# A second norm's statistics as sums, one product for delta*u, and a projection in two column tiles

## The chip, the cores and the metric

The kernel runs on one core of a Trainium2 chip. The metric is the device time of one execution in microseconds (us), median of several runs. A core has five engines, each with its own queue of instructions that it works off in order: TensorE (PE in the profile, with PEld for its weight loads), VectorE (DVE), ScalarE (ACT), GpSimd (POOL) and SyncE (SP), which here only issues DMAs. Engines wait for one another by semaphores. All data is float32.

## The reference, cut to what matters

Two layers follow one another. The first is a Mamba block over a picture of 128 x 128 pixels read as a sequence of 16384 steps, for 4 pictures (the batch), followed by a group norm, a SiLU and a residual. The second norms its input again, and uses that only to get four mixing weights for a filter in the frequency domain.

```python
# layer 0
u = silu(conv(x_in) + conv_b)                       # 256 channels
x_dbl = u @ x_proj_w.T                              # 8 + 16 + 16 = 40 columns
dt, Bm, Cm = split(x_dbl, [8, 24])
delta = softplus(dt @ dt_proj_w.T + dt_proj_b)
h = h * exp(delta * A) + delta * B * u              # scan over 16384 steps, 256 x 16 states
y = einsum('bds,bs->bd', h, C)
...
x = silu(group_norm(out, 4 groups)) + x             # first norm
# layer 1
a = group_norm(concat([x, x]), 32 groups)           # second norm: mean and variance of the line above
weights = softmax(mean(relu(a @ agg_w + agg_b)) @ wg_w.T + wg_b)
out = irfft2(sum_f weights_f * rfft2(x) * rfft2(filtered_f(x))) + 0.5 * x
```

What the change touches is the projection of `u` to 40 columns, the product `delta * u`, and the mean and variance of the second norm. The result of the computation stays the same but for rounding.

## The kernel before

**Tiling.** `block0` cuts each picture into 32 chunks of 512 steps, so 128 chunks `k` in all (`NCH` = 32 for a picture). Per chunk there are 256 channels x 16 states = 4096 state rows, laid out as 32 tiles of 128 partitions x 512 steps. The tiles are called by `(j, r, p)`: `j` is the half of the channels (2), `r` the rotation (4), `p` the group of states (4). Two tiles make a pair, and there are `NP` = 16 pairs per chunk, one for each step of the schedule. So step `n` of the whole program is pair `n % 16` of chunk `n // 16`.

**What one tile costs.** ACT makes `da = exp(delta * A)` (L393). The input `delta*u*B` of the scan is made on POOL for `p` = 1, 2, 3 (`dbu`, L363) and by PE and ACT for `p` = 0 (`bt_act` L304, `dbu_turn` L383). DVE runs the scan over the 512 steps (L412). Then `h` is multiplied by `C`: on DVE (L414) where `by_vector(k, j, r, p)` says so, on POOL (L419) otherwise. ACT copies the last column for the next chunk (`st`, L415 and L420). PE adds the products up to `y` (`sums`, L433), DVE multiplies `y` by the gate (L443).

**The share of h*C.** As `by_vector` stands, DVE multiplies the tiles with `p` = 2 and 3, 16 of 32. In odd chunks it takes one more, (1, 2, 1). In chunks in which the norm of the previous picture runs (`norming(k)`, L338: `k >= 32` and `k % 32` from 2 to 17, so 16 chunks for each of three pictures, 48 in all) DVE takes one less, without (1, 2, 2), which is pair 13.

**Order.** The order is written out by hand. `pre(k)` and `post(k)` list triples of step, phase and function. Step 0 of `pre` is the first pair of the chunk before (`pre` runs one chunk ahead). In each step the phases come in the order of L552: turn, sums, pe, exps, late, act, pool, dbu, early, gate, scans, dve, end. Every engine gets its instructions in that order. What the change touches runs thus, with steps counted within a chunk:

- step 2: `silu_act` (u), and in norming chunks two `norm_act` (L633: SiLU of the first norm, written to PSUM)
- step 3: `xd_mm` (L247: u times the 40 columns), and at the end of the step two `norm_dve` (L637: plus the residual, then the store) each followed by `norm_stats` (L641: `bn_stats`)
- step 4: `xd_act` (L253: the copy of the 40 x 512 result, and the store of B and C to DRAM)
- step 5: `dt_mm` (L267), `xd_turn` (L282: four transposes of 40 x 128), the loads of B and C, and `o_act` (L456, L457) of an earlier chunk
- step 6: `dt_act` (L275: softplus[...]); step 7: `xd_turn_act` (L286), `du_pool` twice on POOL (L312, with a store each); step 8: `du_turn` (L293); step 9 and 16: `rep_load` (the loads of delta and delta*u, each repeated four times over the partitions)

The exponentials for the pairs are spread over this: `exps(n)` puts the first tile of an even pair three steps early, and everything else in the step before its scan.

**The norms.** `finish` runs both norms of one picture beside the chunks of the next picture. `group_norm` is used for the first one (`which` = 0, sums and sums of squares from ACT, L456 and L457) and for the second (`which` = 1, `bn_stats` and `bn_aggr`). The last picture has no chunks left to hide behind. Its `finish` runs in `block1`, the frequency part, where DVE, ACT and POOL have other work.

Of the kernel before, what the change touches and what calls it, by code (L numbers as in the profile page):

```python
# [26 lines left out]
F32 = mybir.dt.float32  # L27
AF = mybir.ActivationFunctionType
ALU = mybir.AluOpType
AX = mybir.AxisListType  # L30
# [3 lines left out]
P = 128  # L34
# [12 lines left out]
def kernel(ctx: ExitStack, tc: tile.TileContext, a: dict, out: bass.AP):  # L47
# [32 lines left out]
    def first_constants(s):  # L80

        s.b1 = col("mlp_b1")
        s.w2 = const("w2", [P, NH, C], a["mlp_w2T"].rearrange("(j p) c -> p j c", p=P))
        s.b2 = col("mlp_b2")
        win = s.win = const("win", [P, 2 * DI], a["in_wT"])
        wck = s.wck = const("wck", [P, KC, DI], a["conv_wT"].partition_broadcast(P))
        s.cb = col("conv_b")
        s.wx = const("wx", [P, NH, NX], a["x_wT"].rearrange("(j p) r -> p j r", p=P))
        s.wdt = const("wdt", [R, DI], a["dt_wT"])
        s.bdt = col("dt_b")  # L90
        s.ident = const("ident", [P, P], a["c_ident"])
# [63 lines left out]
def block0(tc, s):  # L155
    nc, B, NCH, NH, NS, NG, ND, R, NX, KC, HALO, C, L, NF, DI = (
        s.nc, s.B, s.NCH, s.NH, s.NS, s.NG, s.ND, s.R, s.NX, s.KC, s.HALO, s.C, s.L, s.NF, s.DI,
    )
    NT = T // P
    with ExitStack() as ctx:  # L160
        def pool(name, bufs, **kw):
            return ctx.enter_context(tc.tile_pool(name=name, bufs=bufs, **kw))
# [3 lines left out]
        hpool = pool("hb", 4)  # L166
        tiny = pool("tiny", 2)
        dbc = pool("dbc", 2, space=DRAM)
        s.spare = p2
# [14 lines left out]
        def pre(k):  # L184
# [59 lines left out]
            def xd_mm():  # L244
                ps["xd"] = turn_bank(f"xd_{k}")
                for j in range(NH):
                    nc.tensor.matmul(  # L247
                        ps["xd"][0:NX, :], s.wx[:, j, :], d["u"][:, j, :], start=j == 0, stop=j == NH - 1
                    )

            def xd_act():
                xd = d["xd"] = p1.tile([NX, T], F32, tag="xd", name=f"xd_{k}")
                nc.scalar.copy(xd, ps["xd"][0:NX, :])  # L253
                bc = d["bc"] = dbc.tile([2, NS, T], F32, tag="bc", name=f"bc_{k}")
                nc.sync.dma_start(out=bc.rearrange("q s t -> (q s) t"), in_=xd[R:NX, :])

            def bc_load():
                for q, tag in enumerate("BC"):
# [19 lines left out]

            def xd_turn():
                ps["xt"] = turned(f"xdt_{k}")  # L280
                for t in range(NT):
                    nc.tensor.transpose(ps["xt"][:, t, 0:NX], d["xd"][:, t * P : (t + 1) * P], s.ident[0:NX, 0:NX])  # L282

            def xd_turn_act():
                d["xdt"] = p1.tile([P, NT, NX], F32, tag="xdt", name=f"xdt_{k}")
                nc.scalar.copy(d["xdt"], ps["xt"][:, :, 0:NX])  # L286

            def du_turn(h):
                ps["dut"] = turned(f"dut_{k}_{h}")
# [15 lines left out]
                        d["bt"][:, 2 * h + t, :, q, :], src, AF.Copy, scale=d["xdt"][:, 2 * h + t, R + q : R + q + 1]  # L305
                    )

            def du_pool(j):
                if j == 0:
                    d["du"] = p1.tile([P, NH, T], F32, tag="du", name=f"du_{k}")  # L310
                du = d["du"][:, j, :]
                nc.gpsimd.tensor_tensor(du, d["delta"][:, j, :], d["u"][:, j, :], ALU.mult)  # L312
                nc.sync.dma_start(out=d["dd"][1, j * P : (j + 1) * P, :], in_=du)

            def rep_load(j):
                for q, tag in enumerate(("delta", "du")):
# [9 lines left out]
                (5 if k else 7, "act", bc_load), (6, "act", dt_act), (7, "act", xd_turn_act), (7, "pool", partial(du_pool, 0)),  # L326
                (7, "pool", partial(du_pool, 1)), (8, "pe", partial(du_turn, 0)), (9, "act", partial(rep_load, 0)),
# [19 lines left out]
        def by_vector(k, j, r, p):  # L347

            if norming(k):
                return p > 1 and (j, r, p) != (1, 2, 2)  # L350
            return p > 1 or (k % 2 == 1 and (j, r, p) == (1, 2, 1))

        def dbu(u):
# [200 lines left out]
                        f()  # L554


def group_norm(s, io, b, mat, which, stat, at, then):


    nc = s.nc  # L560
    g = {}

    def small(n, m=1):
        g[n] = io.small.tile([P, m], F32, tag=n, name=f"{n}_{which}_{b}")
        return g[n]

    def aggregate():
        mv = small("mv", 2)
        if which:
            nc.vector.bn_aggr(mv, stat().rearrange("p n q -> p (n q)"))  # L570
        else:
            nc.vector.reduce_sum(mv, stat(), axis=AX.X)

    def mean_mm():
        if which == 0:
            mv, q = g["mv"], small("q")
            nc.scalar.activation(q, mv[:, 0:1], AF.Square, scale=1.0 / s.L)
            nc.scalar.mul(q, q, -1.0)
            nc.scalar.mul(mv[:, 0:1], mv[:, 0:1], 1.0 / s.L)
            nc.scalar.activation(mv[:, 1:2], mv[:, 1:2], AF.Identity, scale=1.0 / s.L, bias=q)  # L580
        ps = g["ps"] = io.psum(f"gm_{which}_{b}")
        nc.tensor.matmul(ps[:, 0:1], getattr(s, mat), g["mv"][:, 0:1], start=True, stop=True)

    def spread_act():
        mv = g["mv"]
        nc.scalar.copy(small("mean"), g["ps"][:, 0:1])
        q = small("q")
        nc.scalar.activation(q, mv[:, 0:1], AF.Square, scale=-1.0, bias=g["mean"])
        nc.scalar.activation(q, q, AF.Identity, bias=mv[:, 1:2])

    def var_mm():
        ps = g["ps"] = io.psum(f"gv_{which}_{b}")
        nc.tensor.matmul(ps[:, 0:1], getattr(s, mat), g["q"], start=True, stop=True)

    def root_act():
        nc.scalar.activation(small("rstd"), g["ps"][:, 0:1], AF.Sqrt, bias=s.eps)

    def invert():
        nc.vector.reciprocal(g["rstd"], g["rstd"])
# [8 lines left out]
def finish(s, io, b, first, norm, agg, add="dve"):  # L608

# [6 lines left out]
    def start(mean, rstd):  # L616
        for n in ("scale", "bias"):
            g[n] = io.small.tile([P, 1], F32, tag=n, name=f"{n}_{b}")
        nc.scalar.activation(g["scale"], s.gnw, AF.Identity, scale=rstd)
        nc.scalar.activation(g["bias"], mean, AF.Identity, scale=g["scale"])  # L620
        nc.scalar.activation(g["bias"], g["bias"], AF.Identity, scale=-1.0, bias=s.gnb)
        g["stat"] = io.small.tile([P, NCH, 6], F32, tag="stats1", name=f"stats1_{b}")

    def norm_load(i):
        xr = g["x", i] = io.big.tile([P, T], F32, tag="xr", name=f"xr_{b}_{i}")
# [7 lines left out]
        nc.scalar.activation(g["n", i], g["o", i], AF.Silu, bias=g["bias"], scale=g["scale"])  # L633

    def norm_dve(i):
        o = g["o", i]
        nc.vector.tensor_add(o, g.pop(("n", i)), g.pop(("x", i)))  # L637
        nc.sync.dma_start(out=s.x1flat[b][:, i * T : (i + 1) * T], in_=o)

    def norm_stats(i):  # L640
        nc.vector.bn_stats(g["stat"][:, i, :], g.pop(("o", i)))  # L641

    def middle(mean, rstd):
        g["mean"] = mean
# [51 lines left out]
    def weights_act():  # L696
        nc.scalar.activation(s.wts[b], g["lg"], AF.Identity, scale=g["total"])

    todo = group_norm(s, io, b, "g0", 0, lambda: stats[b], first, start)
# [7 lines left out]
    todo += group_norm(s, io, b, "g1", 1, lambda: g["stat"], c, middle)  # L707
    todo += [(c + 7, "pe", bias_mm), (c + 8, "act", bias_act)]
    for i in range(NCH):
        at = agg(i)  # L710
# [11 lines left out]
def block1(tc, s):  # L722
# [10 lines left out]
    with ExitStack() as ctx:  # L733
# [32 lines left out]

        t1 = norm(NCH - 1)[2] + 14
        todo = defaultdict(list)
        steps = finish(s, io, B - 1, 0, norm, lambda i: (t1 + i - 3, t1 + i, t1 + i, None), "add")
# [289 lines left out]
```

## Time and profile before

| | |
|---|---|
| median of 3 runs | 7132.03 us (7131.95 to 7132.24) |
| the profiled execution | 7134.96 us, of which the span is 7133.1 us |
| DVE busy | 6888.6 us |
| POOL busy | 6892.0 us |
| ACT busy | 6140.8 us |
| PE busy | 5887.2 us |

The span goes from the first to the last instruction of the profiled execution. The remaining 1.9 us lie around it. The chunks of `block0` take the first 6420 us or so, and the frequency part takes the rest. A group of instructions in the profile carries its line in the kernel, the engine, the output and inputs, the shape, the count, and then the busy time and the mean duration of one. On DVE, ACT and POOL a duration reaches over the start of the next instruction, so the distance from start to start is shorter than the duration. Where instructions follow one another without idle time, the distance is the price.

### The profile page before, as it was taken

What the parts mean: (1) busy time and instruction counts of PE and PEld (TensorE: products, weight loads), DVE (VectorE), ACT (ScalarE), POOL (GpSimd) and SP (SyncE); (2) the same over time, 40 slices, a digit from 0 to 9 for tenths busy, and PEclk for the clock granted to TensorE, in tenths of its full rate; (3) what the DMA queues carried; (4) which work ended last, traced back from release to release, by engine and by line L of the source; (5) the groups of instructions that cost most, each with busy time, mean ns of one, the idle gap of its engine ahead of it and who ended that gap; (6) DMA issues with size and microseconds to landing.
All of it is one profiled execution on the core that took longest, in us unless ns stands there. A gap on an engine that the chain in (4) does not pass through costs nothing.

```text
span 7133.1 us, 91388 instructions
## 1 busy us (share of the span) xinstructions
PE 5887.2 (83%) x26708; PEld 2606.0 (37%) x26708; DVE 6888.6 (97%) x7966; ACT 6140.8 (86%) x13658; POOL 6892.0 (97%) x3188
## 2 busy tenths in 40 slices
PE   6888888888887788888888888888888888877899
PEld 2333333323222233333333333333333333326789
DVE  6999999999999999999999999999999999997888
ACT  6888888888888888898888888898888888877887
POOL 6999999999999999999999999999999999997898
PEclk8888888888888889998898899998889899989999
DMA  6666666667777776777777777677777767759977
GB/s 140 159 154 162 159 151 164 160 151 176 180 188 182 182 172 170 180 180 172 195 186 196 188 175 178 168 187 173 197 189 195 190 167 177 172 140 271 274 213 209
DMA packets 909640, 1288.33 MB, mean 181 GB/s; under 512 B 81736, under 2 KB 360912, under 8 KB 909136
## 3 DMA queue, kind: packets, MB, share of 16 engines
q1 hardware_dynamic: 908992, 1282.22, 72.4%
q8 instruction: 210, 3.44, 0.2%
q14 instruction: 294, 2.41, 0.1%
q10 hardware_dynamic: 144, 0.26, 0.0%
HBM read 1025.58 MB, written 256.58 MB: 180 GB/s over the span
## 4 chain that ended last, share of the span: by engine, by line
DVE 44%; ACT 30%; issue 11%; PE 6%; DMA 4%; POOL 3%; SPq 1%; DVEq 0%; ACTq 0%; POOLq 0%
DVE da L412 20%; DVE h L412 12%; ACT da L393 12%; DVE hb L414 5%; ACT L393 3%; DMA rdelta<-dd 2%; ACT L275 2%; ACT delta L275 2%; ACT bt L304 2%; PE y L433 1%; DVE zs L443 1%; POOL hb L363 1%; ACT L242 1%; DVE pr L894 1%; POOL hb L419 1%
## 5 line engine op out<-in xcount | busy, mean ns | idle before, releaser
L363 POOL TENSOR_TENSOR hb<-rdu,rB 128x1536 f32<-128x1536 f32 (+2 forms) x1536 | 3604.8, 2363 | 22.4 <-DMA rdelta<-dd 21.3
L393 ACT ACTIVATE da<-rdelta,amat 128x512 f32<-128x512 f32 x4096 | 2794.1, 700 | 138.3 <-DVE h L412 133.9
L419 POOL TENSOR_TENSOR hb<-h,rC 128x1024 f32<-128x1024 f32 (+1 forms) x1072 | 2434.0, 2273 | 89.1 <-DVE h L412 73.8
L412 DVE TENSOR_TENSOR_SCAN da<-da,st,hb 128x512 f32<-128x512 f32 x1976 | 2419.9, 1267 | 21.4 <-ACT da L393 14.3
L433 PE MATMUL y<-hb,sel 128*32 128x512 f32 x8192 | 1314.2, 717 | 2.9 <-POOL hb L419 2.7
L414 DVE TENSOR_TENSOR hb<-da,rC 128x512 f32<-128x512 f32 x2040 | 1296.3, 674 | 3.0
L412 DVE TENSOR_TENSOR_SCAN h<-da,st,b 128x512 f32<-128x512 f32 x992 | 1258.4, 1269 | 1.8 <-PE b L383 1.6
L412 DVE TENSOR_TENSOR_SCAN h<-da,st,hb 128x512 f32<-128x512 f32 x1000 | 1251.8, 1256 | 1.8 <-ACT da L393 1.8
L383 PE MATMUL b<-ident,bt 128*128 128x128 f32 x4096 | 747.3, 305 | 517.1 <-DVE h L412 391.7
L234 PE MATMUL pp_cv<-xm,wck 128*128 128x512 f32 x2048 | 1013.5, 640 | 1.6 <-ACT xm L217 0.8
L304 ACT ACTIVATE bt<-pt_dut,xdt 128x256 f32<-128x256 f32 x2048 | 839.4, 474 | 184.5 <-PE pt_dut L293 184.3
L383 PEld LDWEIGHTS b<-ident,bt 128*128 128x128 f32 x4096 | 530.8, 154 | 1017.6 <-DVE h L412 691.6
L415 ACT COPY st<-da 128x1 f32<-128x1 f32 x2040 | 273.2, 160 | 474.5 <-DVE hb L414 471.4
L234 PEld LDWEIGHTS pp_cv<-xm,wck 128*128 128x128 f32 x2048 | 395.5, 203 | 651.9 <-issue 422.5
L830 POOL TENSOR_TENSOR wb<-wb,term 128x1040 f32<-128x1040 f32 x192 | 461.3, 2403 | 39.0 <-ACT term L824 29.6
L293 PE MATMUL pt_dut<-ident,du 128*128 128x128 f32 x1024 | 232.1, 337 | 287.7 <-ACT xdt L286 176.3
L429 PE MATMUL y<-u,diag 128*128 128x512 f32 x512 | 303.0, 675 | 187.6 <-DVE zs L443 186.1
L293 PEld LDWEIGHTS pt_dut<-ident,du 128*128 128x128 f32 x1024 | 131.9, 162 | 606.9 <-POOL du L312 478.4
L393 ACT ACT_TABLE_LOAD x262 | 336.1, 1283 | 12.0 <-DMA rdelta<-dd 7.4
L312 POOL TENSOR_TENSOR du<-delta,u 128x512 f32<-128x512 f32 x256 | 318.7, 1266 | 28.1 <-ACT delta L275 28.1
L223 PE MATMUL pp_z<-xm,win 128*128 128x512 f32 x512 | 274.5, 634 | 51.8 <-ACT fq L497 46.2
L267 PE MATMUL pp_dt<-xd,wdt 8*128 8x512 f32 x512 | 284.9, 641 | 33.2 <-ACT pp_o L457 23.5
(160 smaller groups left out, 8095.7 us busy)
## 6 DMA issues: line engine op xcount, KB each, us to landing
rdelta<-dd SPq DMA_DIRECT2D x1024, 256.0 KB, 4.6
rdu<-dd SPq DMA_DIRECT2D x1024, 256.0 KB, 7.4
rC<-bc SPq DMA_DIRECT2D x512, 256.0 KB, 7.4
rB<-bc SPq DMA_DIRECT2D x512, 192.0 KB, 4.7
dd<-delta SPq DMA_DIRECT2D x256, 256.0 KB, 7.2
dd<-du SPq DMA_DIRECT2D x256, 256.0 KB, 5.7
ft<-in_filt_w SPq DMA_DIRECT2D x108, 520.0 KB, 7.2
ob<-o SPq DMA_DIRECT2D x128, 256.0 KB, 2.1
```

Of the source, the lines that this page charges most:

```text
L234: nc.tensor.matmul(ps["cv", j], w, d["xm"][:, t : t + T], start=t == 0, stop=t == KC - 1)
L293: nc.tensor.transpose(ps["dut"][:, 2 * t + j, :], d["du"][:, j, at : at + P], s.ident)
L304: nc.scalar.activation(d["bt"][:, 2 * h + t, :, q, :], src, AF.Copy, scale=d["xdt"][:, 2 * h + t, R + q : R + q + 1])
L312: nc.gpsimd.tensor_tensor(du, d["delta"][:, j, :], d["u"][:, j, :], ALU.mult)
L363: nc.gpsimd.tensor_tensor(hb[:, p : p + n, :], d["du", j][:, m : m + n, :], d["B"][:, p - 1 : p - 1 + n, :], ALU.mult)
L383: nc.tensor.transpose(b[:, t * P : (t + 1) * P], src, s.ident)
L393: nc.scalar.activation(da, d["delta", j][:, m, :], AF.Exp, scale=s.amat[:, c : c + 1])
L412: nc.vector.tensor_tensor_scan(o, das[q], b, init, ALU.mult, ALU.add)
L414: nc.vector.tensor_tensor(hb[:, p + q, :], das[q], d["C"][:, p + q, :], ALU.mult)
L419: nc.gpsimd.tensor_tensor(hb[:, ps, :], h[:, q, :], d["C"][:, ps, :], ALU.mult)
L433: nc.tensor.matmul(y[m * DG : (m + 1) * DG, :], s.sel, d["hb", j, r][:, p, :], start=False, stop=r == NG - 1)
L830: nc.gpsimd.tensor_tensor(wb, wb, u[n].terms[f], ALU.add)
```

## The change

Three things are changed, and one share is moved to go with the first.

- **Second norm.** For the first three pictures, `norm_dve` becomes one `tensor_tensor_reduce`, which adds the residual and also sums up the result over the 512 steps. `bn_stats` is gone. ACT squares the result with a sum (`norm_stats`), one step later, in the act phase of step 4. It writes the squares over the tile of x, which nothing reads any more. `bn_aggr` becomes a `reduce_sum`, and `mean_mm` divides by the length in four small ACT instructions as it does for the first norm. The picture in `block1` keeps `bn_stats` (`sums=False`).
- **Share of h*C.** In odd norming chunks DVE takes tile (1, 2, 2) back from POOL. In the order of instructions that is 24 products of 128x512 that leave POOL and 24 that DVE gets.
- **delta*u.** One POOL product of 128x1024 and one store of 512 KB in place of two of each.
- **Projection.** `wx` is padded with zeros from 40 to 64 columns. The 512 steps are cut in two halves, whose results land on partitions 0 to 63 and 64 to 127 of PSUM, 256 columns each. So the copy to SBUF is 128x256, not 40x512, the store of B and C is two DMAs, `dt_mm` reads all 128 partitions with weights that are zero but for the rows of one half, and `xd_turn` needs two transposes, not four.

```diff
-        s.wx = const("wx", [P, NH, NX], a["x_wT"].rearrange("(j p) r -> p j r", p=P))
-        s.wdt = const("wdt", [R, DI], a["dt_wT"])
+        s.wx = s.own.tile([P, NH, P // 2], F32, tag="wx", name="wx")
+        nc.vector.memset(s.wx, 0.0)
+        nc.sync.dma_start(out=s.wx[:, :, 0:NX], in_=a["x_wT"].rearrange("(j p) r -> p j r", p=P))
+        s.wdt = s.own.tile([P, 2, DI], F32, tag="wdt", name="wdt")
+        nc.vector.memset(s.wdt, 0.0)
+        for h in range(2):
+            nc.sync.dma_start(out=s.wdt[h * P // 2 : h * P // 2 + R, h], in_=a["dt_wT"])
...
                 for j in range(NH):
-                    nc.tensor.matmul(
-                        ps["xd"][0:NX, :], s.wx[:, j, :], d["u"][:, j, :], start=j == 0, stop=j == NH - 1
-                    )
+                    for h in range(2):
+                        o = ps["xd"][h * HP : (h + 1) * HP, 0:TH]
+                        u = d["u"][:, j, h * TH : (h + 1) * TH]
+                        nc.tensor.matmul(o, s.wx[:, j, :], u, start=j == 0, stop=j == NH - 1)
...
-                xd = d["xd"] = p1.tile([NX, T], F32, tag="xd", name=f"xd_{k}")
-                nc.scalar.copy(xd, ps["xd"][0:NX, :])
+                xd = d["xd"] = p1.tile([P, TH], F32, tag="xd", name=f"xd_{k}")
+                nc.scalar.copy(xd, ps["xd"][:, 0:TH])
...
-                    nc.tensor.matmul(
-                        ps["dt", j], s.wdt[:, j * P : (j + 1) * P], d["xd"][0:R, :], start=True, stop=True
-                    )
+                    for h in range(2):
+                        o = ps["dt", j][:, h * TH : (h + 1) * TH]
+                        nc.tensor.matmul(o, s.wdt[:, h, j * P : (j + 1) * P], d["xd"], start=True, stop=True)
...
-                for t in range(NT):
-                    nc.tensor.transpose(ps["xt"][:, t, 0:NX], d["xd"][:, t * P : (t + 1) * P], s.ident[0:NX, 0:NX])
+                for t in range(2):
+                    nc.tensor.transpose(ps["xt"][:, t, :], d["xd"][:, t * P : (t + 1) * P], s.ident)
...
-            def du_pool(j):
-                if j == 0:
-                    d["du"] = p1.tile([P, NH, T], F32, tag="du", name=f"du_{k}")
-                du = d["du"][:, j, :]
-                nc.gpsimd.tensor_tensor(du, d["delta"][:, j, :], d["u"][:, j, :], ALU.mult)
-                nc.sync.dma_start(out=d["dd"][1, j * P : (j + 1) * P, :], in_=du)
+            def du_pool():
+                du = d["du"] = p1.tile([P, NH, T], F32, tag="du", name=f"du_{k}")
+                nc.gpsimd.tensor_tensor(du, d["delta"], d["u"], ALU.mult)
+                nc.sync.dma_start(out=d["dd"][1].rearrange("(j p) t -> p j t", p=P), in_=du)
...
             if norming(k):
-                return p > 1 and (j, r, p) != (1, 2, 2)
+                return p > 1 and (k % 2 == 1 or (j, r, p) != (1, 2, 2))
...
     def aggregate():
         mv = small("mv", 2)
-        if which:
+        if sums:
+            nc.vector.reduce_sum(mv, stat(), axis=AX.X)
+        else:
             nc.vector.bn_aggr(mv, stat().rearrange("p n q -> p (n q)"))
-        else:
-            nc.vector.reduce_sum(mv, stat(), axis=AX.X)
...
     def norm_dve(i):
-        o = g["o", i]
-        nc.vector.tensor_add(o, g.pop(("n", i)), g.pop(("x", i)))
+        o, n = g["o", i], g.pop(("n", i))
+        if sums:
+            total = g["stat"][:, 0, i : i + 1]
+            nc.vector.tensor_tensor_reduce(o, n, g["x", i], 1.0, 0.0, ALU.add, ALU.add, total)
+        else:
+            nc.vector.tensor_add(o, n, g.pop(("x", i)))
         nc.sync.dma_start(out=s.x1flat[b][:, i * T : (i + 1) * T], in_=o)
 
     def norm_stats(i):
-        nc.vector.bn_stats(g["stat"][:, i, :], g.pop(("o", i)))
+        o = g.pop(("o", i))
+        if sums:
+            nc.scalar.activation(g.pop(("x", i)), o, AF.Square, accum_out=g["stat"][:, 1, i : i + 1])
+        else:
+            nc.vector.bn_stats(g["stat"][:, i, :], o)
...
-            (at[2], add, partial(norm_dve, i)), (at[2], "end", partial(norm_stats, i)),
+            (at[2], add, partial(norm_dve, i)), (at[2] + sums, "act" if sums else "end", partial(norm_stats, i)),
```

More of the change, by code (lines that the diff above doesn't have):

```diff
@@ L158, in block0 @@
     )
-    NT = T // P
+    NT, TH, HP = T // P, T // 2, P // 2
     with ExitStack() as ctx:
@@ L168, in block0 @@
         dbc = pool("dbc", 2, space=DRAM)
-        s.spare = p2
+        s.own, s.spare = p1, p2
         psp = pool("psp", 2, space=PSUM)
@@ L246, in xd_mm @@
                 for j in range(NH):
-                    nc.tensor.matmul(
-                        ps["xd"][0:NX, :], s.wx[:, j, :], d["u"][:, j, :], start=j == 0, stop=j == NH - 1
-                    )
+                    for h in range(2):
+                        o = ps["xd"][h * HP : (h + 1) * HP, 0:TH]
+                        u = d["u"][:, j, h * TH : (h + 1) * TH]
+                        nc.tensor.matmul(o, s.wx[:, j, :], u, start=j == 0, stop=j == NH - 1)
             def xd_act():
-                xd = d["xd"] = p1.tile([NX, T], F32, tag="xd", name=f"xd_{k}")
-                nc.scalar.copy(xd, ps["xd"][0:NX, :])
+                xd = d["xd"] = p1.tile([P, TH], F32, tag="xd", name=f"xd_{k}")
+                nc.scalar.copy(xd, ps["xd"][:, 0:TH])
                 bc = d["bc"] = dbc.tile([2, NS, T], F32, tag="bc", name=f"bc_{k}")
-                nc.sync.dma_start(out=bc.rearrange("q s t -> (q s) t"), in_=xd[R:NX, :])
+                rows = bc.rearrange("q s t -> (q s) t")
+                for h in range(2):
+                    nc.sync.dma_start(out=rows[:, h * TH : (h + 1) * TH], in_=xd[h * HP + R : h * HP + NX])
             def bc_load():
@@ L266, in dt_mm @@
                     ps["dt", j] = psum(f"dt_{k}_{j}")
-                    nc.tensor.matmul(
-                        ps["dt", j], s.wdt[:, j * P : (j + 1) * P], d["xd"][0:R, :], start=True, stop=True
-                    )
+                    for h in range(2):
+                        o = ps["dt", j][:, h * TH : (h + 1) * TH]
+                        nc.tensor.matmul(o, s.wdt[:, h, j * P : (j + 1) * P], d["xd"], start=True, stop=True)
             def dt_act():
@@ L280, in xd_turn @@
                 ps["xt"] = turned(f"xdt_{k}")
-                for t in range(NT):
-                    nc.tensor.transpose(ps["xt"][:, t, 0:NX], d["xd"][:, t * P : (t + 1) * P], s.ident[0:NX, 0:NX])
+                for t in range(2):
+                    nc.tensor.transpose(ps["xt"][:, t, :], d["xd"][:, t * P : (t + 1) * P], s.ident)
             def xd_turn_act():
                 d["xdt"] = p1.tile([P, NT, NX], F32, tag="xdt", name=f"xdt_{k}")
-                nc.scalar.copy(d["xdt"], ps["xt"][:, :, 0:NX])
+                src = ps["xt"][:, 0:2, :].rearrange("p t (h r) -> p h t r", h=2)
+                nc.scalar.copy(d["xdt"].rearrange("p (h t) r -> p h t r", h=2), src[:, :, :, 0:NX])
             def du_turn(h):
@@ L325, in pre @@
                 (NP - 2, "pe", z_mm), (NP - 1, "act", z_act), (NP + 2, "act", z_silu), (3, "pe", xd_mm), (4, "act", xd_act), (5, "pe", dt_mm), (5, "pe", xd_turn),
-                (5 if k else 7, "act", bc_load), (6, "act", dt_act), (7, "act", xd_turn_act), (7, "pool", partial(du_pool, 0)),
-                (7, "pool", partial(du_pool, 1)), (8, "pe", partial(du_turn, 0)), (9, "act", partial(rep_load, 0)),
+                (5 if k else 7, "act", bc_load), (6, "act", dt_act), (7, "act", xd_turn_act), (7, "pool", du_pool),
+                (8, "pe", partial(du_turn, 0)), (9, "act", partial(rep_load, 0)),
                 (8, "pool", partial(bt_act, 0, 0, 1)), (9, "act", partial(bt_act, 0, 1, 5)),
@@ L554, in block0, with group_norm @@
                         f()
-def group_norm(s, io, b, mat, which, stat, at, then):
+def group_norm(s, io, b, mat, which, stat, at, then, sums):
     nc = s.nc
@@ L568, in aggregate @@
         mv = small("mv", 2)
-        if which:
+        if sums:
+            nc.vector.reduce_sum(mv, stat(), axis=AX.X)
+        else:
             nc.vector.bn_aggr(mv, stat().rearrange("p n q -> p (n q)"))
-        else:
-            nc.vector.reduce_sum(mv, stat(), axis=AX.X)
     def mean_mm():
-        if which == 0:
+        if sums:
             mv, q = g["mv"], small("q")
@@ L605, in group_norm, with finish @@
     ]
-def finish(s, io, b, first, norm, agg, add="dve"):
+def finish(s, io, b, first, norm, agg, add="dve", sums=True):
     nc, NCH, C, L, NF = s.nc, s.NCH, s.C, s.L, s.NF
@@ L621, in start @@
         nc.scalar.activation(g["bias"], g["bias"], AF.Identity, scale=-1.0, bias=s.gnb)
-        g["stat"] = io.small.tile([P, NCH, 6], F32, tag="stats1", name=f"stats1_{b}")
+        shape = [P, 2, NCH] if sums else [P, NCH, 6]
+        g["stat"] = io.small.tile(shape, F32, tag="stats1", name=f"stats1_{b}")
     def norm_load(i):
@@ L635, in norm_dve @@
     def norm_dve(i):
-        o = g["o", i]
-        nc.vector.tensor_add(o, g.pop(("n", i)), g.pop(("x", i)))
+        o, n = g["o", i], g.pop(("n", i))
[4 more added lines that the diff above has]
+            nc.vector.tensor_add(o, n, g.pop(("x", i)))
         nc.sync.dma_start(out=s.x1flat[b][:, i * T : (i + 1) * T], in_=o)
     def norm_stats(i):
-        nc.vector.bn_stats(g["stat"][:, i, :], g.pop(("o", i)))
+        o = g.pop(("o", i))
+        if sums:
+            nc.scalar.activation(g.pop(("x", i)), o, AF.Square, accum_out=g["stat"][:, 1, i : i + 1])
+        else:
+            nc.vector.bn_stats(g["stat"][:, i, :], o)
     def middle(mean, rstd):
@@ L697, in weights_act @@
         nc.scalar.activation(s.wts[b], g["lg"], AF.Identity, scale=g["total"])
-    todo = group_norm(s, io, b, "g0", 0, lambda: stats[b], first, start)
+    todo = group_norm(s, io, b, "g0", 0, lambda: stats[b], first, start, True)
     for i in range(NCH):
@@ L703, in finish @@
             (at[0], "pe", partial(norm_load, i)), (at[1], "act", partial(norm_act, i)),
-            (at[2], add, partial(norm_dve, i)), (at[2], "end", partial(norm_stats, i)),
+            (at[2], add, partial(norm_dve, i)), (at[2] + sums, "act" if sums else "end", partial(norm_stats, i)),
         ]
     c = at[2] + 5
-    todo += group_norm(s, io, b, "g1", 1, lambda: g["stat"], c, middle)
+    todo += group_norm(s, io, b, "g1", 1, lambda: g["stat"], c, middle, sums)
     todo += [(c + 7, "pe", bias_mm), (c + 8, "act", bias_act)]
@@ L768, in block1 @@
         todo = defaultdict(list)
-        steps = finish(s, io, B - 1, 0, norm, lambda i: (t1 + i - 3, t1 + i, t1 + i, None), "add")
+        steps = finish(s, io, B - 1, 0, norm, lambda i: (t1 + i - 3, t1 + i, t1 + i, None), "add", False)
         for at, phase, f in steps:
```

## The prediction

> **What bounds the kernel now.** I read the busy row of the page first, then the stretches of single chunks, then the groups of DVE, and last the order in time of ACT within one chunk.
>
> ```profile
> span 7133.1 us, 91388 instructions
> PE 5887.2 (83%) x26708; PEld 2606.0 (37%) x26708; DVE 6888.6 (97%) x7966; ACT 6140.8 (86%) x13658; POOL 6892.0 (97%) x3188
> ...
> core 0: us, PE busy (x) PEld busy (x) DVE busy (x) ACT busy (x) POOL busy (x), PEclk, DMA share, GB/s
> 632.00:680.80 48.80, 41.03 (x152) 15.52 (x152) 48.77 (x51) 41.70 (x94) 47.93 (x23) 0.84 0.65 155
> 680.80:729.50 48.70, 38.82 (x152) 14.20 (x152) 48.70 (x52) 42.03 (x96) 48.70 (x23) 0.89 0.69 161
> 2031.10:2081.40 50.30, 38.88 (x150) 13.85 (x149) 50.27 (x54) 43.25 (x95) 50.05 (x24) 0.86 0.73 184
> 2081.40:2131.70 50.30, 42.58 (x153) 15.67 (x152) 50.27 (x54) 43.25 (x95) 50.06 (x24) 0.81 0.75 185
> ```
>
> Two engines at 97% leave open which one bounds. The stretches answer it. The first two are chunk-long stretches without a norm, the last two are norming chunks (40 and 41). In all four DVE is idle for at most 0.03 us. POOL has 0.8 us in every second plain stretch and 0.25 us in a norming chunk, and ACT has 7 us. So a chunk lasts as long as DVE's work, 48.75 us plain and 50.30 us norming, and POOL stands 0.5% behind it. What is taken from POOL alone is worth nothing; what is taken from DVE is worth its price until POOL or a late ACT takes over.
>
> ```profile
> L412 DVE TENSOR_TENSOR_SCAN da<-da,st,hb 128x512 f32<-128x512 f32 x1976 | 2419.9, 1267 | 21.4 <-ACT da L393 14.3 <-POOL hb L363 4.1 <-issue 2.9
> L414 DVE TENSOR_TENSOR hb<-da,rC 128x512 f32<-128x512 f32 x2040 | 1296.3, 674 | 3.0
> ...
> 2043.52 1.28 DVE L637 TENSOR_TENSOR of<-pp_n,xr 128x512 f32<-128x512 f32 x2
> 2044.71 1.27 DVE L641 BATCH_NORM_STATS2 stats<-of 128x6 f32<-128x512 f32 x2
> 2045.90 1.26 DVE L412 TENSOR_TENSOR_SCAN h<-da,st,b 128x512 f32<-128x512 f32 x1
> ```
>
> The groups give durations (674 ns for a product), the times from start to start give prices: two additions 1.19 us, two statistics 1.19 us, so 0.595 us each. The same reading gives 0.59 for a product on DVE, 1.18 for a scan. On POOL it gives 2.31 for 128x1024 and 2.44 for the two du products.
>
> The third reading is ACT in the steps behind the norm (chunk 40), against the scan that waits for it:
>
> ```profile
> 2047.46 0.57 ACT L253 COPY xd<-pt_xd 40x512 f32<-40x512 f32 x1
> 2048.38 0.69 ACT L393 ACTIVATE da<-rdelta,amat 128x512 f32<-128x512 f32 x1 [0.34 <-DVE h L412]
> ...
> 2051.32 0.16 ACT L415 COPY st<-da 128x1 f32<-128x1 f32 x1 [0.34 <-DVE hb L414]
> 2051.91 0.16 ACT L415 COPY st<-da 128x1 f32<-128x1 f32 x1 [0.43 <-DVE hb L414]
> 2051.97 1.31 ACT L393 ACTIVATE da<-rdelta,amat 128x512 f32<-128x512 f32 x2
> ...
> 2058.86 1.30 ACT L393 ACTIVATE da<-rdelta,amat 128x512 f32<-128x512 f32 x2
> ...
> 2060.06 2.44 DVE L412 TENSOR_TENSOR_SCAN da<-da,st,hb 128x512 f32<-128x512 f32 x2
> ```
>
> ACT waits for DVE three times, 0.34 + 0.34 + 0.43 us, the last time at the copies of pair 5. From there it works without a wait through softplus and two table loads to the exponentials of pair 9 (2058.86). The first of those ends at 2058.86 + 0.69 = 2059.55, and DVE wants it at 2060.06. So ACT is only 0.51 us ahead there. The rule: if DVE gets more than that ahead of ACT, it waits at pair 9.
>
> [...] here L457, a square between exponentials, has no table load.
>
> **The change part by part.** There are 48 norming chunks with two norm pieces each.
>
> *Statistics, DVE.* Gone: two `bn_stats`, 1.19 us. Added: what the addition with a sum costs above the plain one, and two reads of the accumulator. The trace shows neither. The first is bounded by 0 (it reads the same two streams) and by 0.585 (the rate of the scan); I take 0[...]. [...]
>
> *Share of h*C.* In 24 odd chunks DVE gets a product, 0.59 us, at pair 13, behind the place in question. Mean 0.30 us per norming chunk. POOL loses 1.22 us in these.
>
> *Squares, ACT.* Two of 128x512 with their reads. L457 does the same at 0.515 us from start to start, its read at 0.09, so 2 x 0.61 = 1.21 us. They stand in step 4 behind `xd_act`, and wait for an addition that ended 3 us before, so for nothing. Behind them on ACT are one exponential, `o_act`, an early exponential, the copies of pair 5, then the softplus stretch. The xd copy shrinks by 256 columns: copies of 512 (L228) and 160 (L286) take 0.477 and 0.183 from start to start, so 0.84 ns per column and 0.21 us.
>
> *The sum at pair 9.* Before, ACT reaches the exponential of 2048.38 at 2048.04. Now it gets there at 2048.04 + 1.21 - 0.21 = 2049.04 and need not wait. Then 2.60 us of work lead to the first copy of pair 5 (2051.64), two copies take 0.16, and the exponentials of pair 7 begin at 2051.80, 0.17 earlier than before. DVE would be 1.04 earlier. The difference of 0.87 goes against the 0.51 us of lead, so DVE waits about 0.36 us at pair 9, and 0.68 of the 1.04 us remain. The other places have more lead: 1.68 us at pair 4, 1.35 at pair 5 (both in front of the squares), 1.5 at pair 7, 1.0 at pair 8. As ACT limits, a dearer addition costs nothing up to 0.18 us each.
>
> A norming chunk then takes 50.30 - 0.68 + 0.30 = 49.92 us on average, and 48 x 0.38 = 18 us are gained.
>
> *POOL.* delta*u as one product saves 2.44 - 2.31 = 0.13 us in every chunk. POOL's work in a norming chunk becomes 49.92 in even and 48.70 in odd ones, 49.3 on average, below DVE's 49.9. The even chunks lie above DVE's share by about 0.3 us; the scans stand at least 1.4 us behind the POOL products they read in chunks 36 to 47, which carries it to the next chunk. Without the moved share POOL would be the bound at 49.92 throughout. In plain chunks POOL's saving is hidden by DVE: nothing. Only late in the run does DVE wait for POOL (4.1 us in all at L363): about 1 us.
>
> *delta*u, the stores.* SP issues both halves one behind the other before the loads of delta anyway, and the loaded delta*u lies there 4 us before its use, so the merged store costs nothing. If that cover went, it would be one store of 256 KB later, a few us per chunk.
>
> *Projection.* PE is 83% busy and behind nobody here: `dt_mm` ends at 2051.5 and softplus starts at 2054.6. Whether the two column tiles run together is not seen in this trace, and is worth 0 to 1 us of 1.9 us on PE per chunk that nobody waits for (DVE's waits for PE are 43 us at the start and little else). The second store of B and C, 64 KB in all, is issued with 2 us to spare. The two memsets at the start hold up SP's loads of constants by up to 1 us, once.
>
> *End of the second norm.* `bn_aggr` (0.92 us) becomes a sum (0.13), and four ACT instructions of 0.1 to 0.2 us come in step 8, behind the exponentials of pair 9. Three times: 1 to 2 us gained.
>
> Sum: 18 + 1 + 1.5 - 0.5 = 20 us, 0.28% of the profiled 7134.96, and of the median of 7132.03, which lies 2.9 us below that one execution. Forecast 7111 us.
>
> **The rivals.**
>
> *ACT keeps up.* If the squares are cheaper or hide in waits, DVE keeps the whole 1.04 us: 48 x (1.04 - 0.30) = 36, with the rest 38 us, 7094 us. For it: ACT has 7 us idle per chunk. Against it: that idle time lies in other steps.
>
> *ACT costs more.* The squares read SBUF; the SiLU of the norm, which also does, takes 0.75 us from start to start (with two operands per partition that the square lacks). At 0.75 the squares cost 0.47 more, DVE keeps 0.21 of the 1.04 us, the moved share takes 0.30, and nothing is left: 7118 to 7134 us, no difference to be told.
>
> *The addition with a sum runs at the scan's rate.* Slower: each costs 0.585 more, so DVE's chunk is 50.30 - 1.04 + 1.17 + 0.30 = 50.73, and 48 x 0.43 = 20 us are lost, 7150 us with the 2 us of the rest. The place is step 3 of the norming chunks; with the moved share in it, loss begins at 0.37 us more per addition. For it: one known operation of this engine runs so, and this one is not in the trace. [...]
>
> **How the numbers follow.** Forecast 0.50 (7104 to 7118), ACT keeps up 0.22 (7092 to 7103), ACT costs more 0.16, slow addition 0.12. Predicted is 7111. The range leaves out the slow addition and little else: 7093 to 7132. A measurement can tell 0.2%, 14 us, from no change: faster is below 7117.8, slower above 7146.3. Faster is the forecast but for its upper end and the second case, 0.69; same 0.19; slower 0.12.
>
> **What would show it.** DVE's rows should have 96 additions of about 680 ns and 96 reads below 0.1 us, and 24 more products. Norming chunks should last 49.6 to 49.7 us even and about 50.2 odd, with idle time of 0.3 to 0.4 us before the scan of pair 9, ended by ACT's L393; plain chunks should stay at 48.7 to 48.8. The forecast is wrong if that idle time is missing (then the chunk is shorter), if additions take over a microsecond, or if POOL has no idle time left in the norming chunks.

## The result

| | before | changed |
|---|---|---|
| median of 7 runs | 7131.95 us | 7107.63 us |
| lowest and highest | 7130.78 and 7133.24 | 7105.26 and 7110.93 |
| profiled execution | 7134.96 us | 7106.15 us |
| its span | 7133.1 us | 7104.4 us |

The ratio is 0.9966, with a 95% interval of 0.9957 to 0.9976. The change is 24 us faster, or 0.34%. The two profiled executions lie 29 us apart. That is more than the medians show, because the one of before was 3.0 us above its median and the other 1.5 us below.

The page of the changed kernel, busy row first, and then the stretches of chunks 40 (even) and 41 (odd), in which the norm runs:

```profile
span 7104.4 us, 93142 instructions
PE 5622.1 (79%) x27476; PEld 2693.8 (38%) x27476; DVE 6847.9 (96%) x7992; ACT 6168.4 (87%) x13862; POOL 6845.8 (96%) x3036
...
2026.81:2076.31 49.50, 36.54 (x155) 14.60 (x155) 49.20 (x54) 43.97 (x99) 49.30 (x23) 0.89 0.74 188
2076.31:2126.26 49.95, 40.05 (x160) 16.72 (x159) 49.69 (x55) 44.03 (x99) 49.95 (x22) 0.88 0.76 186
```

The columns of the stretches are the length, then busy time of PE, PEld, DVE, ACT and POOL. Both chunks lasted 50.30 us before. DVE now has 0.3 us of idle time in each, where it had 0.03. So something else than DVE's own work sets part of the chunk. The timelines of DVE and ACT in chunk 40 say what it is:

```profile
2039.81 0.68 DVE L647 CUSTOM_DVE_ANT_0 of<-pp_n,xr 128x512 f32<-128x512 f32 x1
2040.42 0.08 DVE L647 DVE_READ_ACCUMULATOR2_ANT stats<- 128x1 f32 x1
2040.42 1.27 DVE L419 TENSOR_TENSOR_SCAN h<-da,st,b 128x512 f32<-128x512 f32 x1
...
2053.40 1.25 DVE L419 TENSOR_TENSOR_SCAN h<-da,st,hb 128x512 f32<-128x512 f32 x1
2054.92 2.47 DVE L419 TENSOR_TENSOR_SCAN da<-da,st,hb 128x512 f32<-128x512 f32 x2 [0.26 <-ACT da L400]
```

```profile
2043.14 0.36 ACT L259 COPY xd<-pt_xd 128x256 f32<-128x256 f32 x1
2043.41 0.62 ACT L655 ACTIVATE xr<-of 128x512 f32<-128x512 f32 x1
2043.93 0.19 ACT L655 ACTIVATION_READ_ACCUMULATOR xr<-of 128x1 f32 x1
2044.03 0.62 ACT L655 ACTIVATE xr<-of 128x512 f32<-128x512 f32 x1
2044.55 0.19 ACT L655 ACTIVATION_READ_ACCUMULATOR xr<-of 128x1 f32 x1
2044.64 0.68 ACT L400 ACTIVATE da<-rdelta,amat 128x512 f32<-128x512 f32 x1
...
2047.13 0.20 ACT L422 COPY st<-da 128x1 f32<-128x1 f32 x2
2047.31 1.30 ACT L400 ACTIVATE da<-rdelta,amat 128x512 f32<-128x512 f32 x2
...
2054.20 1.30 ACT L400 ACTIVATE da<-rdelta,amat 128x512 f32<-128x512 f32 x2
```

Three things are to be seen. The addition with a sum takes 0.61 us from start to start, and its accumulator read takes nothing: the scan starts at the same 2040.42 as the read, and so does the next instruction behind all 96 reads of the trace. ACT no longer waits at the copies of pair 5 (2047.13), where it waited 0.34 and 0.43 us before. And the scan of pair 9 at 2054.92 waits 0.26 us for the exponential that ACT starts at 2054.20. That is the place the prediction named.

POOL and SP have a wait that is new, in the loads of delta*u:

```profile
L370 POOL TENSOR_TENSOR hb<-rdu,rB 128x1536 f32<-128x1536 f32 (+2 forms) x1536 | 3613.0, 2370 | 39.9 <-DMA rdelta<-dd 20.7 <-DMA rdu<-dd 13.0 <-DMA x<-x 2.2
...
SPq L327 <- DMA dd<-du: 31.1, 57, 4.4
```

The first row is a group with the releasers of its idle time. The second is from the list of waits of SP's queue: total us, times, longest. Before, POOL waited 0.9 us for delta*u, and SP 2.6 us (2 times) for its store to land.

### The profile page after: what moved, and what is told of

Read it like the earlier page. It is cut to its first block, busy times and chain, and to the rows that moved or that the text cites. A ratio compares the mean times of both kernels' runs of the same rounds, so it can differ in the third digit from the quotient of the medians.

```text
span 7104.4 us, 93142 instructions
## 1 busy us (share of the span) xinstructions
PE 5622.1 (79%) x27476; PEld 2693.8 (38%) x27476; DVE 6847.9 (96%) x7992; ACT 6168.4 (87%) x13862; POOL 6845.8 (96%) x3036
## 4 chain that ended last, share of the span: by engine, by line
ACT 32%; DVE 28%; POOL 15%; issue 10%; PE 6%; DMA 5%; SPq 2%; DVEq 0%; ACTq 0%; POOLq 0%
DVE da L419 13%; ACT da L400 12%; POOL hb L370 8%; DVE h L419 7%; POOL hb L426 6%; ACT L400 3%; DVE hb L421 3%; DMA rdelta<-dd 2%; ACT bt L313 2%; ACT L247 2%; PE y L440 2%; ACT delta L283 2%; ACT L283 2%; ACT zs L247 1%; POOL du L319 1%
## 5 line engine op out<-in xcount | busy, mean ns | idle before, releaser
L370 POOL TENSOR_TENSOR hb<-rdu,rB 128x1536 f32<-128x1536 f32 (+2 forms) x1536 | 3613.0, 2370 | 39.9 <-DMA rdelta<-dd 20.7
L419 DVE TENSOR_TENSOR_SCAN da<-da,st,hb 128x512 f32<-128x512 f32 x2000 | 2449.0, 1268 | 38.0 <-ACT da L400 26.2
L440 PE MATMUL y<-hb,sel 128*32 128x512 f32 x8192 | 1242.6, 681 | 4.8 <-POOL hb L426 2.9
L419 DVE TENSOR_TENSOR_SCAN h<-da,st,hb 128x512 f32<-128x512 f32 x976 | 1223.0, 1255 | 1.4 <-ACT da L400 1.4
L390 PE MATMUL b<-ident,bt 128*128 128x128 f32 x4096 | 723.2, 298 | 449.1 <-DVE h L419 325.5
L302 PE MATMUL pt_dut<-ident,du 128*128 128x128 f32 x1024 | 207.8, 337 | 402.5 <-POOL du L319 393.1
L277 PE MATMUL pp_dt<-xd,wdt 128*128 128x256 f32 x1024 | 298.3, 417 | 150.2 <-ACT pp_o L464 141.5
L319 POOL TENSOR_TENSOR du<-delta,u 128x1024 f32<-128x1024 f32 x128 | 301.2, 2353 | 29.8 <-ACT delta L283 28.3
```

What stands on the lines that cost most here:

```text
L302: nc.tensor.transpose(ps["dut"][:, 2 * t + j, :], d["du"][:, j, at : at + P], s.ident)
L319: nc.gpsimd.tensor_tensor(du, d["delta"], d["u"], ALU.mult)
L370: nc.gpsimd.tensor_tensor(hb[:, p : p + n, :], d["du", j][:, m : m + n, :], d["B"][:, p - 1 : p - 1 + n, :], ALU.mult)
L390: nc.tensor.transpose(b[:, t * P : (t + 1) * P], src, s.ident)
L419: nc.vector.tensor_tensor_scan(o, das[q], b, init, ALU.mult, ALU.add)
L440: nc.tensor.matmul(y[m * DG : (m + 1) * DG, :], s.sel, d["hb", j, r][:, p, :], start=False, stop=r == NG - 1)
```

## The experiments

All comparisons are with the changed kernel at 7107.6 us. The kernel of before gave 7132.06 to 7132.46 us in the same sessions. Chunk lengths are distances between the first scans of neighbouring chunks in each trace.

**Squares later.** If ACT is late because of the squares, they belong where ACT waits. In step 11 it waits for PE anyway (1.30 us in chunk 40 of the changed kernel). The end of the second norm moves by 5 steps, since the last squares come later.

```diff
-            (at[2], add, partial(norm_dve, i)), (at[2] + sums, "act" if sums else "end", partial(norm_stats, i)),
+            (at[2], add, partial(norm_dve, i)), (at[2] + 8 * sums, "act" if sums else "end", partial(norm_stats, i)),
...
-    c = at[2] + 5
+    c = at[2] + (10 if sums else 5)
```

> The changed kernel with ACT's two squares in step 11 rather than step 4, in front of a wait of ACT of 1.3 us (and the end of the second norm 5 steps later). Theory (ACT is late at pair 9 because of the squares): DVE's idle time of 0.26 us before the scan of pair 9 in norming chunks is gone, even chunks last 49.2 us and odd ones 49.7 us, 12 us less in 48 chunks, 7093 to 7098 us. Rival (POOL bounds next): POOL's mean of 49.3 us with its parity holds the even chunks at 49.5, and only 3 to 6 us are gained. Rival (DVE alone bounds, the squares cost nothing): 7107.6 within 2 us.

Measured: 7102.23 us (7100.97 to 7106.35). The chunks did what the theory said, 49.14 us even and 49.59 odd, with no wait at pair 9. But only 5 us of the 12 that were expected were kept. The trace has the place of the loss, in the chunk behind the norming ones, here on DVE's timeline:

```profile
2530.26 1.27 DVE L421 TENSOR_TENSOR hb<-da,rC 128x512 f32<-128x512 f32 x2
2537.16 0.16 DVE L606 RECIPROCAL rstd<-rstd 128x1 f32<-128x1 f32 x1 [5.63 <-ACT rstd L603]
2537.24 1.26 DVE L419 TENSOR_TENSOR_SCAN h<-da,st,b 128x512 f32<-128x512 f32 x1
```

A reciprocal of 128x1 stands in DVE's queue in front of the scans and waits 5.63 us for the root on ACT, which at that step comes behind the SiLUs. That chunk lasts 55.5 us in all three pictures. So the number that was to confirm the theory came out low through a second effect of the edit, and this asked for a cleaner one.

**Squares later, end kept.** Only the last two squares of a picture stay in step 4, so that the end of the norm need not move.

```diff
-            (at[2], add, partial(norm_dve, i)), (at[2] + sums, "act" if sums else "end", partial(norm_stats, i)),
+            (at[2], add, partial(norm_dve, i)), (at[2] + (8 if i < NCH - 2 else 1) * sums, "act" if sums else "end", partial(norm_stats, i)),
```

> The changed kernel with the squares in step 11 for the first 30 pieces of a picture, and in step 4 for the last two, so that the end of the second norm stays where the change has it. Theory (the run before it lost what it gained at the moved end of the norm, 5.6 us of DVE's wait for the root in each of three pictures): norming chunks last 49.14 and 49.59 us and the chunk behind them stays below 50 us, so 45 chunks x 0.36 = 16 us less than the changed kernel's 7107.6, 7090 to 7093. Rival (late squares cost as much elsewhere, whatever the end of the norm): 7100 to 7104 as in the run before.

Measured: 7087.31 us (7086.19 to 7088.43), ratio to before 0.9935 with 0.9923 to 0.9948. This is the fastest kernel of the study, 20 us below the changed one. Its stretches for chunks 40 and 41, in the same columns as above, then DVE at pair 9:

```profile
2023.35:2072.49 49.14, 37.46 (x163) 14.99 (x162) 49.10 (x55) 44.05 (x99) 49.00 (x23) 0.96 0.77 189
2072.49:2122.08 49.59, 36.93 (x157) 14.85 (x156) 49.59 (x56) 43.98 (x99) 49.59 (x22) 0.90 0.78 187
...
2049.94 1.26 DVE L419 TENSOR_TENSOR_SCAN h<-da,st,hb 128x512 f32<-128x512 f32 x1
2051.12 2.44 DVE L419 TENSOR_TENSOR_SCAN da<-da,st,hb 128x512 f32<-128x512 f32 x2
```

ACT does the same work (44.0 us per chunk), in another place, and each norming chunk is 0.36 us shorter. The wait for ACT at pair 9 was thus worth 0.36 us per chunk, 0.26 of idle time and some 0.1 more around it. The chunk behind the norming ones lasts 48.4 to 49.6 us now, so the moved end explains the loss of the run before. The median came out 3 us below what was expected: in the two traces the norming chunks give 16 us, and the chunks behind them 3 us more, for which no reason was found.

**The old projection.** The changed kernel with the projection of before. The edit takes back the whole projection; the diff shows the copy.

```diff
...
-                xd = d["xd"] = p1.tile([P, TH], F32, tag="xd", name=f"xd_{k}")
-                nc.scalar.copy(xd, ps["xd"][:, 0:TH])
+                xd = d["xd"] = p1.tile([NX, T], F32, tag="xd", name=f"xd_{k}")
+                nc.scalar.copy(xd, ps["xd"][0:NX, :])
...
```

> The changed kernel with the projection of before: 40 x 512 results, one store of B and C, eight-row weights, four transposes. Theory (ACT binds at pair 9, and the projection's smaller copy gives it 0.21 us in front of that): DVE's idle time in norming chunks grows from 0.26 to 0.47 us, even and odd chunks become 49.70 and 50.15, 48 x 0.21 = 10 us more, 7115 to 7120 us. Rival (the projection is hidden work and worth nothing): 7107.6 within 2 us.

Measured: 7118.57 us (7114.94 to 7122.55). Chunks last 49.72 and 50.17 us, each 0.22 us longer. DVE's idle time at pair 9:

```profile
2052.67 1.28 DVE L410 TENSOR_TENSOR_SCAN h<-da,st,hb 128x512 f32<-128x512 f32 x1
2054.30 2.47 DVE L410 TENSOR_TENSOR_SCAN da<-da,st,hb 128x512 f32<-128x512 f32 x2 [0.34 <-ACT da L391]
```

The idle time grew less (0.26 to 0.34) than the chunk did, so the length of the chunk is the better measure of such a wait. The theory stands: the smaller copy is worth 11 us here.

**The new projection alone**, on the kernel of before. With the padded weights and the full tile of ones, 0.906 KB per partition of SBUF are left and a pool needs 1 KB, so half of that tile goes.

```diff
...
-        s.ones = cpool.tile([P, P], F32, tag="ones", name="ones")
+        s.ones = cpool.tile([P, P // 2], F32, tag="ones", name="ones")
...
-                xd = d["xd"] = p1.tile([NX, T], F32, tag="xd", name=f"xd_{k}")
-                nc.scalar.copy(xd, ps["xd"][0:NX, :])
+                xd = d["xd"] = p1.tile([P, TH], F32, tag="xd", name=f"xd_{k}")
+                nc.scalar.copy(xd, ps["xd"][:, 0:TH])
...
```

> The kernel of before with the new projection alone (to make room for it, a constant tile of ones has half its columns, and the small instruction that reads it four times in the run is done in two halves). Theory (without the squares DVE is the bound and ACT leads by 0.5 us at pair 9): plain and norming chunks stay at 48.75 and 50.30 us, 7132 within 3 us. Rival (the shorter copy is worth 0.2 us in every chunk): 20 us less.

Measured: 7133.38 us (7127.77 to 7135.46), ratio 1.0000 with 0.9992 to 1.0009; norming chunks at 50.30 us. The same edit is worth nothing here and 11 us beside the squares. What an edit off the bound is worth depends on whether another edit uses the room that it makes.

**Without the moved share.** The changed kernel, with tile (1, 2, 2) left to POOL in odd chunks too.

```diff
-                return p > 1 and (k % 2 == 1 or (j, r, p) != (1, 2, 2))
+                return p > 1 and (j, r, p) != (1, 2, 2)
```

> The changed kernel without the moved share of h*C: in odd norming chunks POOL keeps tile (1, 2, 2). Theory (POOL at 49.92 us of work in every norming chunk becomes the bound): norming chunks last 49.9 to 50.0 us, DVE waits for POOL in them, 9 to 14 us more than the changed kernel, 7117 to 7122 us. Rival (DVE bounds and POOL has room): all norming chunks last 49.5 us, 10 us less, 7097 us.

Measured: 7112.46 us (7108.38 to 7114.60), 5 us more, outside both expectations. The spread of the runs overlaps with that of the changed kernel, but the norming chunks of the two traces say the same: 4.7 us more in the sum of all 48. The trace has both theories, one after the other. In the second picture's norm the first six chunks last 49.50 to 49.51 us, the next 49.67, and then they last 49.80 to 49.93, up to the last one, in which the norm ends. The stretches of chunk 36 and of chunks 45 and 46, and DVE at the start of chunk 45:

```profile
1823.69:1873.20 49.51, 40.85 (x160) 17.43 (x159) 49.22 (x55) 44.05 (x99) 49.51 (x22) 0.84 0.78 188
2270.71:2320.57 49.86, 38.30 (x158) 15.74 (x156) 49.33 (x55) 43.93 (x99) 49.86 (x23) 0.87 0.76 186
2320.57:2370.44 49.87, 38.92 (x162) 16.38 (x161) 49.34 (x54) 43.82 (x99) 49.87 (x23) 0.89 0.75 182
...
2272.22 1.28 DVE L419 TENSOR_TENSOR_SCAN h<-da,st,hb 128x512 f32<-128x512 f32 x1 [0.25 <-POOL hb L370]
```

POOL never rests (49.51 of 49.51, 49.86 of 49.86), yet at first DVE does not wait for it. How far POOL is behind can be read from its delta*u product, one per chunk: in the norm of the second picture it starts 24.45 us after the chunk's first scan in the first chunk, and 0.38 us later in each chunk that follows. At 26.9 us a lead of 2.5 us is used up, and from there on DVE waits for POOL in each chunk (0.19 to 0.31 us).

**The moved share alone**, on the kernel of before.

```diff
-                return p > 1 and (j, r, p) != (1, 2, 2)
+                return p > 1 and (k % 2 == 1 or (j, r, p) != (1, 2, 2))
```

> The kernel of before with the moved share alone: in odd norming chunks DVE takes tile (1, 2, 2) from POOL. Theory (a product that stands right behind the scan it reads costs 0.71 us, in the pair of two products each costs 0.59, so the moved product adds only 0.45 to 0.47 us): odd norming chunks last 50.75 us, even ones 50.30, 24 x 0.46 = 11 us more, 7143 us. Rival (it adds its price of 0.59 us): 50.89 us, 14 us more. Rival (relief of POOL is worth something): below 7140 us.

Measured: 7140.95 us (7138.53 to 7145.81), ratio 1.0014 with 1.0007 to 1.0020. Odd chunks last 50.75 us, even ones 50.30: the product costs 0.45 us, though its price from start to start is 0.59. DVE at pair 13 of this kernel, an even chunk and then an odd one:

```profile
2071.52 1.25 DVE L412 TENSOR_TENSOR_SCAN da<-da,st,hb 128x512 f32<-128x512 f32 x1
2072.81 0.69 DVE L414 TENSOR_TENSOR hb<-da,rC 128x512 f32<-128x512 f32 x1
2073.42 1.27 DVE L412 TENSOR_TENSOR_SCAN h<-da,st,b 128x512 f32<-128x512 f32 x1
...
2120.64 2.44 DVE L412 TENSOR_TENSOR_SCAN da<-da,st,hb 128x512 f32<-128x512 f32 x2
2122.99 1.27 DVE L414 TENSOR_TENSOR hb<-da,rC 128x512 f32<-128x512 f32 x2
2124.17 1.27 DVE L412 TENSOR_TENSOR_SCAN h<-da,st,b 128x512 f32<-128x512 f32 x1
```

A single product reads the scan just in front of it and starts 1.29 us after that scan's start; where two scans and two products follow one another, the step is 1.18. The second product takes that away. In the trace of before the step is 1.29 to 1.31 us at all 88 single products, and 1.18 at 944 of the 976 pairs.

**The share in thirds**, on the kernel with late squares and the end kept.

```diff
-                return p > 1 and (k % 2 == 1 or (j, r, p) != (1, 2, 2))
+                return p > 1 and (k % 3 == 1 or (j, r, p) != (1, 2, 2))
```

> The kernel with late squares (end kept), with the share moved in every third norming chunk, not every second. Theory (the lead of POOL, about 3 us, is used up slowly: POOL's mean is 49.92 - 1.22 / 3 = 49.51, DVE's 49.14 + 0.45 / 3 = 49.29, so 0.22 us of lead go per chunk and last some 13 of 16 chunks): 48 x 0.08 = 3 to 4 us less than with every second, 7083 to 7086 us. Rival (POOL bounds before): 7087 to 7095 us.

Measured: 7092.11 us (7086.17 to 7097.31). A miss: after five to seven chunks the chunks with the moved tile last 50.0 to 50.2 us instead of 49.59. At pair 13 of these, the pair of the moved tile, DVE waits for POOL's product with C, as here in chunk 40:

```profile
2065.59 2.47 DVE L419 TENSOR_TENSOR_SCAN da<-da,st,hb 128x512 f32<-128x512 f32 x2 [0.31 <-POOL hb L426]
```

POOL's lead is used up sooner than worked out, because I compared means. With two unmoved chunks in a row, POOL's delta*u product slips from 24.33 to 25.81 us after the first scan (chunks 68 to 70); with the tile moved in every second chunk it stays between 24.3 and 25.1 from the second norming chunk on. In the next group of three it reached 26.36, and DVE waited. So the swing within three chunks takes most of the lead, and the slow loss that I worked out has little left to use up.

**delta*u in three forms.** First two products and two stores again in the changed kernel, then one product with two stores, then the kernel of before with one product and one store alone.

```diff
-                nc.sync.dma_start(out=d["dd"][1].rearrange("(j p) t -> p j t", p=P), in_=du)
+                for j in range(NH):
+                    nc.sync.dma_start(out=d["dd"][1, j * P : (j + 1) * P, :], in_=du[:, j, :])
```

(This is the second of the three.)

> The changed kernel with delta*u in two products and two stores again; all else as changed. Theory (the merged store comes later): the loads of delta*u no longer wait for a store of 512 KB, so POOL's waits for them, 13 us in the changed kernel, go back below 3 us, DVE's waits for POOL from 10 to about 4 us, and the time falls by 4 to 7 us against the changed kernel's 7107.6, although POOL works 0.13 us longer per chunk. Rival (the smaller POOL work helps, since POOL is only 0.5% behind DVE): the time rises by 3 to 10 us. Rival (delta*u is hidden either way): within 2 us.

> The changed kernel with delta*u as one product, but stored as two halves of 256 KB. Theory (the merged store is late because it is long): the half that the first loads need lands about 1 us earlier, so POOL's waits for delta*u fall from 13 us to some 5 us and the time by 2 to 5 us. Rival (it is late because the product ends later for the first half, by 1.1 us): waits and time stay as in the changed kernel, 7107.6 within 2 us.

> The kernel of before with delta*u as one product and one store alone. Theory (POOL's work is hidden by DVE, and the loads of delta*u have to wait for the longer store): 0 to 6 us more than 7132, with POOL's waits for delta*u above 8 us, and norming chunks at 50.30 us. Rival (POOL, 0.5% behind DVE, sets part of the time): 3 to 10 us less.

| | median | SP waits for the store | POOL waits for delta*u | DVE's scans into `da` wait for POOL |
|---|---|---|---|---|
| changed kernel | 7107.63 us | 31.1 us | 13.0 us | 10.0 us |
| two products, two stores | 7107.77 us | 3.5 us | 3.0 us | 4.4 us |
| one product, two stores | 7109.12 us | 5.7 us | 27.4 us, 20.7 of it once at the start | 6.0 us |
| before with one and one | 7131.81 us | 30.9 us | none in the list | 5.7 us |

The waits moved as the theory of the late store says, except in the last kernel, where POOL did not wait at all. The time moved by less than 2 us in all three, and the last has a ratio of 0.9999 with 0.9990 to 1.0007. So the third expectation of the first run holds: delta*u is hidden either way. The merged store makes SP wait some ten times as long, and that shows in no median.

## Why the prediction was right

- **What bounds.** DVE's work sets the chunk, POOL stands just behind it: the projection alone and the product alone, which relieve ACT, PE and POOL, are worth nothing, and the share alone costs time although it relieves POOL. One of my own signs of being wrong did appear: POOL has no idle time left in chunk 41 (49.95 of 49.95 us). It did not bind there, for the late squares shortened the chunks to 49.14 and 49.59 us with the same work on POOL.
- **The place where ACT takes over.** Confirmed, by the wait at pair 9 in the trace and by its removal (the late squares). I forecast about 0.36 us per chunk, and moving the squares gains 0.36 us per chunk. That the two agree so closely is luck: DVE gets 0.13 us further ahead than I took and ACT is 0.17 us faster, and these two errors cancel in the wait.
- **What DVE saves.** Mis-sized. The 1.04 us of the forecast are the 1.19 us of the two statistics less a price for the two reads of the accumulator. That price was only an estimate of mine, and so was it that the sum would add nothing to the addition: the trace of before shows neither. The read takes 0, so DVE gets 1.17 us ahead, not 1.04. The addition itself is 0.61 us, as taken within 0.02. As ACT limits at pair 9, this made the wait longer and the even chunks no shorter.
- **What ACT takes.** From the copies of pair 1 to the exponentials of pair 7 it was to be 0.17 us faster than before, and is 0.34 us (14.83 us before, 14.49 after). From there to the exponentials of pair 9, through softplus and two table loads of 1.28 us each, both kernels take 6.89 us. The squares at 0.61 us each were exact. What I had wrong were two steps that stood in front of a wait before: the copy of xd and the last exponential before the copies of pair 5. I put them down with their durations, 0.57 and 0.71 us, since no start of a next instruction followed at once. In the changed kernel nothing waits there, and from start to start such a copy of 512 columns is 0.48 us (80 copies in the trace of before have another instruction right behind) and the exponential 0.61. This term alone explains why 0.80 us per even chunk remained, not 0.68: what remains is the lead at pair 9 (0.51 as read; 0.48 if the scan can start 0.72 us after ACT begins the two exponentials, as it does in the changed kernel) and what ACT gains (0.34), 0.82 us in all.
- **The moved share.** Mis-sized: 0.45 us, not 0.59, for the reason that the run with the share alone shows.
- **Sum for the norming chunks.** 24 x (50.30 - 49.50) + 24 x (50.30 - 49.95) = 27.6 us, where I had 18. That the forecast of the total was only 3 us off is thus in part luck: these chunks gave 10 us more, and other parts of the sum gave less.
- **End of the second norm.** I put down 1 to 2 us for it. They are not seen: the three chunks in which it ends are 1.2 us shorter in all, of which 3 x 0.35 is what every odd norming chunk has.
- **POOL.** I said that without the moved share POOL would bind at 49.92 us throughout. It does so only in the second half, since its lead from the plain chunks carries the first half. So the share is worth 5 us here, not the 9 to 14 that I expected of that run.
- **delta*u.** Worth nothing, as said, but not for the reason given. That the merged store costs nothing was read off the order of SP's queue and one stretch; the loads of the first half do wait for the whole store now.
- **What was given back.** Between the two profiled executions the 48 norming chunks are 29.3 us shorter (the first and the last of a picture differ from the rest). The 41 chunks behind them take 2012.7 us where they took 2008.5, so 4.2 us are lost, and all else is 3.6 us shorter. That makes the 28.7 us between the two spans; the medians are closer because these two executions lie above and below theirs. The loss goes with the second norm: behind the norms, the kernels that have it as sums (with its end in place) take 2009.7 to 2013.4 us, and those that don't 2007.6 to 2009.5. This rests on one trace of each kernel, and where the time is lost was not found.
- **The rivals.** The slow addition is ruled out by its 0.61 us. "ACT costs more" is ruled out by the squares' 0.61 us. "ACT keeps up" is what the kernel with late squares makes true: I gave it 7094 us, and it is 7087 us, because DVE saves more and the share costs less than I took. A rival that I did not name is the clock that TensorE is granted, 0.90 before and 0.93 after. It rises just so with the projection alone (0.93), and that leaves the time as it was.

## What to carry over

Work that is moved off the bounding engine has to go where its new engine waits, not just where that engine has idle time on average: the same two squares cost 0.36 us per chunk in step 4 and nothing in step 11. Look up how far each helper is ahead of the bound at every step. The least lead is what an edit may use. Price a step that stands in front of a wait by the distance from start to start of the same step elsewhere, not by its duration (for a copy of 512 columns 0.48 and not 0.57 us). And an edit that looks worthless alone (the shorter copy) may be what pays for another. When an edit moves a chain of small dependent steps, look for what stands behind its last wait in the queue of the bounding engine (scans, behind a reciprocal that waited 5.63 us).

## What the hardware showed beside that

- The addition with a sum costs DVE 0.61 us for 128x512, one operand in PSUM, and its accumulator read 0 us from start to start (80 ns of duration, beside the next instruction). On ACT the same read takes 0.09 us.
- On DVE a product that stands right behind the scan it reads starts 1.29 us after that scan's start where a single product follows, and 1.18 where two scans and two products follow one another (the run with the moved share alone).
- The two column tiles of the projection run side by side: the two matmuls of a pair start 7 ns apart and the next pair 209 ns later, where a matmul of 512 columns took 429 ns from start to start before. PE is busy for 244.5 us with it before (512 instructions of 600 ns) and 139.1 us after (1024 of 392 ns). Only ACT's copy of xd waited for it, once in each trace (1.2 us before, 0.8 us after).

Here are the groups of before and of the changed kernel for the last point:

```profile
L247 PE MATMUL pt_xd<-u,wx 128*40 128x512 f32 x512 | 244.5, 600 | 0.7 <-ACT u L239 0.7
L255 PE MATMUL pt_xd<-u,wx 128*64 128x256 f32 x1024 | 139.1, 392 | 0.9 <-ACT u L244 0.9
```
